# A graph-attention layer with experts: a second gathered row per lane moved into the feature stage, edge flags turned once, and last groups of three and two blocks

## The chip, the cores and the metric

The kernel runs on one core of one Trainium2 chip. The metric is the device time of one execution in microseconds (us), the median over runs. Times inside an execution come from one profiled execution.

## The reference, cut to what matters

Layer normalisation of `x` (30000 x 256), then graph attention over 510,000 edges that are sorted by destination, then a residual sum, and after a second normalisation a shared MLP and four experts of which the best two per row are used. The part that the change touches is the attention:

```python
feat_all = jnp.einsum('ni,rhid->rnhd', inputs, conv_weights)   # 8 relations, 4 heads of 64
feat_src_e = feat_all[edge_type, edge_src]
el = jnp.sum(feat_src_e * attn_l[edge_type], axis=-1)
er = jnp.sum(feat_all[edge_type, edge_dst] * attn_r[edge_type], axis=-1)
e = leaky_relu(el + er, 0.2)
ex = jnp.exp(e - segment_max(e, edge_dst)[edge_dst])
alpha = ex / segment_sum(ex, edge_dst)[edge_dst]
h = segment_sum(alpha[..., None] * feat_src_e, edge_dst)
```

Each edge needs one row of 260 floats (4 heads of 64 features and one attention term), found by its source node and relation.

## The kernel before, in words

The program has two stages; the engines' orders are written out by hand in both (`manual_schedule`), so every engine runs its instructions in the order of the Python loops.

**The feature stage** goes over NT = 235 tiles of 128 nodes. For a tile TensorE makes five column groups (`group`, matmuls L304), ScalarE copies three of them out of PSUM and VectorE two (L306), and SyncE stores the 1 MB of feature rows to `feat` in DRAM (`store`, L318). PSUM holds six such groups. In slots between the groups, `aside` takes one step of a list of side work, `side`: first `edge_records`, then `places`, then `expert_weights`.

`places` goes over the NBLK = 252 blocks of edges in 21 batches of GB = 12. A block has 2048 edges, 128 lanes (partitions) of U = 16 consecutive edges. In each lane the edge with the lowest feature row is found (key, minimum, mark; L534 to L540) and exchanged with the first edge of the lane (L543 to L550); the mark is kept so that the attention stage can exchange the scores alike. `places` also makes the flags of where a destination begins and ends; their ends are turned from partitions into rows by two TensorE instructions a batch (L580, L581), copied by ScalarE (L583) and stored to `thr_d`. A batch takes nine slots; two slots of a tile are used when `places` runs.

`first_rows` then gathers row 0 of every lane of every block early, during the feature stage: one indirect DMA by GpSimd per block (L625), into `fr`, and a plain DMA of three blocks back to DRAM into `stage` (L620). It begins at tile BT + 2 = 178 of 235. The gather may only read `feat` below tile BT = 176; if any lane's lowest row lies above it, a flag makes the program compute everything again in a general form. In the text such a row is called an early row.

**The attention stage** goes over the 252 blocks and one last block of UL = 18 edges a lane. Iteration t has six slots, c = 0 to 5, and works on several blocks: it loads block t + 2 (`load`), gathers block t + 1 (`gather`: SyncE reads row 0 from `stage`, L954, and GpSimd gathers the other 15 rows by 15 indirect DMAs, L956, into a ring `ft` of four blocks), computes the scores of block t in slot 1 (`scores`, L1060 to L1067: add, leaky ReLU, `exchange` L1051 to L1055, two scans) and their softmax in slot 5 (`softmax`, L1092 to L1095 and `exchange` again), and weighs and sums block t - 1 (`weigh` L1109, `sums` L1116, `finish` L1134 to L1137). Between them stand `turn_ends` (TensorE, L987, waits for the scans), `across` (VectorE), `turn_back` (TensorE) and the exponentials (ScalarE, L1101 and L1102).

Every four finished blocks (T = 4) form a group for the experts. Its 22 steps go into a list, `todo`, of which one is taken in each slot: normalise (`spread`, `scale`, L737 to L747), turn (L755), the layers (L811, L836), gates (L763 to L806), and `last` (TensorE L864 to L867, then VectorE adds in the next slot, L870). 253 blocks give 63 groups of four and a last one of a single block.

Of the kernel before, what the change touches and what calls it, by code (L numbers as in the profile page):

```python
# [21 lines left out]
P = 128  # L22
D = 256
R = 8
# [22 lines left out]
WI, WD, WA, WP, W1 = 0, U, 2 * U, 3 * U, 5 * U  # L47
# [9 lines left out]
def kernel(  # L57
# [47 lines left out]
    stage = dram.tile([NBLK * P, H * HW], F32, name="stage")  # L105
# [115 lines left out]
    with ExitStack() as cx:  # L221
# [263 lines left out]
        BT = 3 * NT // 4  # L485
        count = {"ready": 0, "sent": 0}
        low = gp.tile([P, NBLK], I32, name="low")
        lowc = gp.tile([P, NBLK], I32, name="lowc")

        def places(cl):  # L490


            GB = 12
# [14 lines left out]
            rcs = {}  # L508

# [15 lines left out]
            for k, (b0, n) in enumerate(batches):  # L525
# [4 lines left out]
                key = kp.tile([P, GB, U], F32, name="key", bufs=1)[:, :n]  # L530
                km = kp.tile([P, GB], F32, name="km", bufs=1)[:, :n]
                x = rc[:, :, :U, :3].rearrange("p b u f -> p b f u")
                mark = of[:, :, WA:WA + U]
                nc.vector.scalar_tensor_tensor(key, rc[:, :, :U, 0], float(U),  # L534
                                               iu[:, None, :].to_broadcast([P, n, U]), op0=ALU.mult, op1=ALU.add)
                nc.vector.tensor_reduce(km, key, AX.X, ALU.min)
                yield
                if done:
                    done()
                nc.vector.tensor_tensor(mark, key, km[:, :, None].to_broadcast([P, n, U]), op=ALU.is_equal)  # L540
                m3 = mark[:, :, None, :].to_broadcast([P, n, 3, U])
                t3 = kp.tile([P, GB, 3, U], F32, name="t3", bufs=1)[:, :n]
                nc.vector.tensor_mul(t3, x, m3)  # L543
                yield
                for f in range(3):
                    nc.vector.copy_predicated(x[:, :, f, 1:], o[:, :, WA + 1:WA + U],
                                              x[:, :, f, 0:1].to_broadcast([P, n, U - 1]))
                yield
                with nc.allow_low_precision(reason="integers below 2 ** 24"):
                    nc.vector.tensor_reduce(x[:, :, :, 0], t3, AX.X, ALU.add)  # L550
                yield
# [3 lines left out]
                nc.gpsimd.tensor_copy(low[:, b0:b0 + n], rc[:, :, 0, 0])  # L555
                nc.gpsimd.tensor_scalar_min(lowc[:, b0:b0 + n], rc[:, :, 0, 0], float(BT * P * R - 1))
                nc.gpsimd.tensor_copy(o[:, :, WI:WI + U], rc[:, :, :U, 0])
                count["ready"] = b0 + n
# [19 lines left out]

                ps = pf.tile([P, 512], F32, name="ps")[:n, :2 * P]
                nc.tensor.transpose(ps[:, :P], a1[:, :, U - 1], ident)  # L580
                nc.tensor.matmul(ps[:, P:], a2[:, :, 1], turned, start=True, stop=True)  # L581
                thr = kp.tile([GB, 2 * P], F32, name="thr")[:n]
                nc.scalar.copy(thr, ps)  # L583
# [8 lines left out]
                def done(o=o, d16=d16, thr=thr, b0=b0, n=n):  # L592
                    nc.sync.dma_start(thr_d[b0:b0 + n].rearrange("b i p -> b (i p)"), thr)
                    nc.sync.dma_start(rk_d[b0:b0 + n].rearrange("b p w -> p b w"), o)
                    nc.sync.dma_start(dk_d[b0 * CAP:(b0 + n) * CAP].rearrange("(b p u) -> p b u", p=P, u=U), d16)
            yield
            done()

            exc = gp.tile([P, 1], F32, name="exc")
            nc.vector.tensor_reduce(exc, low, AX.X, ALU.max)  # L600
# [6 lines left out]
            yield  # L607
            both = gp.tile([1, 2], F32, name="both")
            nc.vector.tensor_reduce(both[:, 0:1], exr, AX.X, ALU.max)
            nc.vector.tensor_scalar(both[:, 0:1], both[:, 0:1], float(BT * P * R), None, op0=ALU.is_ge)  # L610
# [3 lines left out]
        def first_rows():  # L614

            n, kept = 3, []
            fp = cl.enter_context(tc.tile_pool(name="first", bufs=3))

            def keep(b0, m, fr):
                nc.sync.dma_start(stage[b0 * P:(b0 + m) * P, :].rearrange("(b p) f -> p b f", p=P), fr[:, :m])  # L620
            for b0 in range(0, NBLK, n):
                m = min(n, NBLK - b0)
                fr = fp.tile([P, n, H * HW], F32, name="fr")
                for b in range(m):
                    nc.gpsimd.indirect_dma_start(  # L625
                        out=fr[:, b], out_offset=None, in_=feat[0:BT * P * R, :],
                        in_offset=bass.IndirectOffsetOnAxis(ap=lowc[:, b0 + b:b0 + b + 1], axis=0))
                    if b == n // 2 and kept:
                        keep(*kept.pop())
                    count["sent"] += 1  # L630
                    yield
                kept.append((b0, m, fr))
            while kept:
                keep(*kept.pop(0))

        with tc.manual_schedule():
# [49 lines left out]
            for m in range(lead, NT - 1):  # L686
                for g in range(NG):
# [4 lines left out]
                    if g == 2 or g == 4 and len(side) < 3:  # L692
                        aside()
                    if m >= BT + 2:
                        fetched = min(fetched + 1.03 * NBLK / ((NT - BT - 2) * NG), 3)
                        while fetched >= 1 and count["sent"] < count["ready"]:
                            next(ahead)
                            fetched -= 1
# [176 lines left out]
    with ExitStack() as cx:  # L875
# [170 lines left out]
        def exchange(s, x):  # L1046

            if not s.own:
                return
# [387 lines left out]
```

## Time and profile before

| what | value |
|---|---|
| median of 3 runs | 6604.08 us (6603.03 to 6612.37) |
| the profiled execution | 6606.58 us, of which the span of the instructions is 6604.9 us |
| mean granted TensorE clock | 0.971 |
| TensorE, VectorE, ScalarE, GpSimd busy | 92%, 79%, 52%, 62% of the span |
| last feature matmul (L304) ends | 1741.3 us after the span's start |
| first and last gather of the attention stage (L956) | 1759.2 and 6521.7 us |
| scores of the first and last block (L1060) | 1779.7 and 6524.5 us |

Busy shares are averages over both stages, and matmuls overlap their neighbours in the records, so a TensorE that is busy 9 tenths is not at its peak. An idle time stands with the instruction that follows it, and the releaser is what ended the wait. [...]

### The profile page before, as it was taken

The numbers are of one execution on the slowest core, as the hardware profiler recorded it, in microseconds if no ns is written. First come the engines' busy times: TensorE is split into PE (matmuls) and PEld (weight loads), VectorE is DVE, ScalarE is ACT, GpSimd is POOL, SyncE is SP. The second block draws the span as 40 slices with busy tenths as digits, with TensorE's granted clock in tenths as the row PEclk, the third lists the DMA queues.
The fourth block names the chain that finished last, engine by engine and source line by source line (L and its number), as shares of the span: only waits on it lengthen the run. The fifth ranks groups of instructions, "written<-read, shape, count | busy, mean of one in ns | idle before, by whom it ended". The sixth has DMA issues, their size and how long they took to land. (4 is left out here: it accounts for less than half of the span.)

```text
span 6604.9 us, 97530 instructions
## 1 busy us (share of the span) xinstructions
PE 6063.8 (92%) x25827; PEld 3894.0 (59%) x25828; DVE 5250.5 (79%) x13699; ACT 3411.6 (52%) x8777; POOL 4077.6 (62%) x4382
## 2 busy tenths in 40 slices
PE   9999999999789889999889999999998999989988
PEld 5555555555456666666666666666666666666665
DVE  5555667644488888898888888888888888888885
ACT  2222222222256656666566665666656666666664
POOL 1111111166677777777777777777777777777773
PEclk9999999999899999999999999999999999999999
DMA  6666777799855555555555555555555555555552
GB/s 228 227 208 200 226 238 225 232 342 328 273 159 160 164 165 163 158 163 163 162 167 159 163 163 162 165 161 163 163 161 164 163 163 163 161 164 163 163 160 80
DMA packets 764818, 1214.73 MB, mean 184 GB/s; under 512 B 242730, under 2 KB 603149, under 8 KB 734045
## 3 DMA queue, kind: packets, MB, share of 16 engines
q1 hardware_dynamic: 568813, 668.72, 31.5%
q0 software_dynamic: 194400, 539.40, 29.3%
q8 instruction: 210, 3.44, 0.2%
q14 instruction: 355, 2.91, 0.1%
q10 hardware_dynamic: 1040, 0.26, 0.0%
HBM read 821.54 MB, written 386.43 MB: 183 GB/s over the span
## 5 line engine op out<-in xcount | busy, mean ns | idle before, releaser
L956 POOL DMA_INDIRECT ft<-feat,rk x3798 | 3606.5, 950 | 1168.9 <-issue 396.0
L1116 PE MATMUL po<-ft,oh 128*128 128x260 f32 x8100 | 2197.1, 408 | 139.8 <-DVE ho L1137 130.2
L1116 PEld LDWEIGHTS po<-ft,oh 128*128 128x128 f32 x8100 | 1525.1, 201 | 437.9 <-issue 199.2
L304 PE MATMUL ps<-w,xT 128*128 128x448 f32 (+1 forms) x4700 | 1713.6, 519 | 1.7 <-DMA w<-_L_gnn_conv_weights_dram 1.7
L1109 DVE TENSOR_TENSOR ft<-ft,p 128x768 f32<-128x768 f32 x1518 | 1292.1, 851 | 89.0 <-ACT ft L1102 85.8
L1043 ACT ACTIVATE oh<-icol,rk 128x128 f32<-128x128 f32 x4032 | 1327.9, 389 | 0.0
L304 PEld LDWEIGHTS ps<-w,xT 128*128 128x128 f32 x4700 | 874.0, 190 | 688.0 <-issue 600.2
L306 ACT COPY fo<-ps 128x448 f32<-128x448 f32 (+1 forms) x711 | 378.3, 532 | 1065.2 <-PE ps L304 969.5
L1044 ACT ACTIVATE oh<-oh 128x384 f32<-128x384 f32 x1518 | 741.1, 488 | 48.0
L1020 PEld LDWEIGHTS <-ohT 128*128 128x128 bf16 x4050 | 378.3, 158 | 405.5 <-issue 331.7
L1033 DVE TENSOR_REDUCE e<-ere 128x16 f32<-128x384 f32 (+1 forms) x1012 | 561.3, 555 | 34.6
L1031 DVE TENSOR_TENSOR ere<-pe,rk 128x384 f32<-128x384 f32 x1008 | 550.7, 546 | 1.5 <-PE pe L1020 1.5
L1101 ACT ACTIVATE p<-e 128x64 f32<-128x64 f32 (+1 forms) x253 | 70.2, 277 | 850.0 <-DVE e L1055 839.2
L811 PE MATMUL ph<-xT,v 128*128 128x512 f32 (+1 forms) x1024 | 490.7, 603 | 1.6 <-ACT h L812 1.3
L1020 PE MATMUL pe<-erp,ohT 128*128 128x96 bf16 x4050 | 439.1, 233 | 56.6 <-DVE ohT L1003 55.3
L306 DVE COPY fo<-ps 128x448 f32<-128x448 f32 (+1 forms) x464 | 242.4, 527 | 215.5 <-PE ps L304 212.3
L293 DVE COPY xT<-ptr 128x256 f32<-128x256 f32 x229 | 96.9, 423 | 378.9 <-PE ptr L291 377.1
L625 POOL DMA_INDIRECT fr<-feat,lowc x252 | 239.5, 951 | 191.3 <-DMA stage<-fr 82.4
L1003 DVE TENSOR_SCALAR ohT<-dr,rowid 128x2064 bf16<-128x2064 int16 (+1 forms) x253 | 323.5, 1279 | 0.0
L273 POOL TENSOR_TENSOR xb<-xg,hb 128x1024 f32<-128x1024 f32 (+1 forms) x59 | 142.0, 2406 | 278.3 <-DMA xg<-in_x_dram 144.1
L987 PE MATMUL t<-ident,fb 128*8 128x128 f32 x506 | 103.6, 289 | 205.5 <-DVE fb L1066 205.4
L555 POOL COPY low<-rcb 128x12 int32<-128x12 int32 x21 | 4.1, 197 | 445.3 <-DVE rcb L550 371.2
(217 smaller groups left out, 6979.4 us busy)
## 6 DMA issues: line engine op xcount, KB each, us to landing
feat<-fo SPq DMA_DIRECT2D x234, 1040.0 KB
dr<-dk_d SPq DMA_DIRECT2D x252, 516.0 KB
ft<-feat,rk POOLq DMA_INDIRECT x3798
stage<-fr SPq DMA_DIRECT2D x84, 390.0 KB
ft<-stage SPq DMA_DIRECT2D x252, 130.0 KB
xt<-xb_d SPq DMA_DIRECT2D x253, 128.0 KB
out_dram<-og SPq DMA_DIRECT2D x253, 128.0 KB
xb_d<-xb SPq DMA_DIRECT2D x58, 512.0 KB
```

The costliest lines, as they stand in the source:

```text
L304: nc.tensor.matmul(ps, t["xT"][:, k, :], w[:, k, c0:c1], start=k == 0, stop=k == 1)
L306: eng(t["fo"][:, h0:h1, :HD], ps[:, :n].rearrange("p (a d) -> p a d", d=HD))
L811: nc.tensor.matmul(ps[:, :self.w], lhs, rhs, start=i == 0, stop=i == len(pairs) - 1)
L956: nc.gpsimd.indirect_dma_start(out=s.ft[:, u].rearrange("p h d -> p (h d)"), out_offset=None, in_=feat[:, :], in_offset=bass.IndirectOffse ...
L1003: nc.vector.tensor_scalar(ohT[:, :3 * s.dw].rearrange("n (i e) -> n i e", i=3), s.dr[:, :, :s.dw], rowid[:, t:t + 1], None, op0=ALU.is_equal)
L1020: nc.tensor.matmul(pe[:, u - u0].rearrange("p f r -> p (f r)"), s.ov[:, u, :], s.erp.rearrange("n h k r -> n (h k r)"), start=True, stop=True)
L1031: nc.vector.tensor_mul(ere, s.pe[:, :u1 - u0], s.th[:, u0:u1, None, :].to_broadcast([P, u1 - u0, H * 3, R]))
L1033: nc.vector.tensor_reduce(s.e[:, :, u0:u1].rearrange("p h u -> p u h"), ere.rearrange("p u (h k) r -> p u h (k r)", h=H), AX.X, ALU.add)
L1043: nc.scalar.activation(s.oh[:, u, :], icol, AF.Abs, bias=s.nd[:, u:u + 1])
L1044: nc.scalar.activation(s.oh[:, u0:u1], s.oh[:, u0:u1], AF.Relu, bias=1.0, scale=-1.0)
L1109: nc.vector.tensor_mul(fc, fc, pc[:, :, None].to_broadcast([P, (u1 - u0) * H, HD]))
L1116: nc.tensor.matmul(s.po.rearrange("n h d -> n (h d)"), s.oh[:, u, :], s.ft[:, u].rearrange("p h d -> p (h d)"), start=u == 0, stop=u == s. ...
```

## The change

- **A second early row in every other block.** In blocks with an even number, `places` finds the second lowest row too, exchanges it into place 1 of the lane, and keeps a second mark (16 words more in each row of `rk_d`). `first_rows` gathers 252 first rows and 126 second rows, 378 in all, in pairs (NS = 2), through four buffers of two blocks where there were three of three, and stores each pair as one contiguous piece per partition. It begins at tile FIRST = 141, at a rate that spreads the 378 over the tiles up to the last but one, and the limit on the rows that a gather may read rises with its place (`rows_there`), some six tiles behind the tile then being made.
- In the attention stage an even block reads two rows from `stages` and gathers 14; an odd one reads one and gathers 15. `exchange` is called twice in `scores` and twice in `softmax` for even blocks; for odd ones the second call returns at once.
- **`places` in denser slots.** A batch has 11 steps where it had nine, and three slots of a tile are used where there were two.
- **Ends of the flags turned once.** The two end columns of each batch are copied by GpSimd into `ends`, and turned at the end of `places` by two TensorE instructions for each 128 blocks.
- **Last groups.** The last groups of the experts have three and two blocks where they had four and one, and from iteration 252 on two steps are taken in each slot.
- The zeroing of `fbs` moves from ahead of the attention stage into its iteration 0.

```diff
-WI, WD, WA, WP, W1 = 0, U, 2 * U, 3 * U, 5 * U
+WI, WD, WA, WP, W1 = 0, U, 2 * U, 4 * U, 6 * U
...
-        BT = 3 * NT // 4
+        NF = (NBLK, (NBLK + 1) // 2)
+        FIRST = NT * 3 // 5
+        RATE = 1.02 * sum(NF) / (NT - 1 - FIRST)
+        GB = 12
...
+        def rows_there(i, b0):
+
+            at = b0 - b0 % GB if i == 0 else NBLK + b0 - b0 % (GB // 2)
+            return min(NT - 2, int(FIRST + at / RATE) - 6) * P * R
...
+                nc.gpsimd.memset(o[:, :, WA + U:WA + 2 * U], 0)
+                for i in range(2):
+
+                    v = rc[:, ::i + 1, i:U]
+                    m, w = (n + i) // (i + 1), U - i
...
+                    nc.vector.scalar_tensor_tensor(key, v[:, :, :, 0], float(U),
+                                                   iu[:, None, :w].to_broadcast([P, m, w]), op0=ALU.mult, op1=ALU.add)
+                    nc.vector.tensor_reduce(km, key, AX.X, ALU.min)
+                    yield
...
+                    nc.vector.tensor_tensor(mark, key, km[:, :, None].to_broadcast([P, m, w]), op=ALU.is_equal)
...
+                    nc.vector.tensor_mul(t3, x, mark[:, :, None, :].to_broadcast([P, m, 3, w]))
...
+                    for f in range(3):
+                        nc.vector.copy_predicated(x[:, :, f, 1:], marki[:, :, 1:],
+                                                  x[:, :, f, 0:1].to_broadcast([P, m, w - 1]))
...
+                        nc.vector.tensor_reduce(x[:, :, :, 0], t3, AX.X, ALU.add)
...
-                ps = pf.tile([P, 512], F32, name="ps")[:n, :2 * P]
-                nc.tensor.transpose(ps[:, :P], a1[:, :, U - 1], ident)
-                nc.tensor.matmul(ps[:, P:], a2[:, :, 1], turned, start=True, stop=True)
-                thr = kp.tile([GB, 2 * P], F32, name="thr")[:n]
-                nc.scalar.copy(thr, ps)
+                nc.gpsimd.tensor_copy(ends[:, 0, b0:b0 + n], a1[:, :, U - 1])
+                nc.gpsimd.tensor_copy(ends[:, 1, b0:b0 + n], a2[:, :, 1])
...
+            for b0 in range(0, NBLK, P):
+
+                n = min(P, NBLK - b0)
+                ps = pf.tile([P, 512], F32, name="ps")[:n, :2 * P]
+                nc.tensor.transpose(ps[:, :P], ends[:, 0, b0:b0 + n], ident)
+                nc.tensor.matmul(ps[:, P:], ends[:, 1, b0:b0 + n], turned, start=True, stop=True)
...
+            fp = cl.enter_context(tc.tile_pool(name="first", bufs=4))
...
+            for i, n in enumerate(NF):
+                for b0 in range(0, n, NS):
+                    m = min(NS, n - b0)
+                    fr = fp.tile([P, NS, H * HW], F32, name="fr")
+                    for b in range(m):
+                        nc.gpsimd.indirect_dma_start(
+                            out=fr[:, b], out_offset=None, in_=feat[0:rows_there(i, b0 + b), :],
+                            in_offset=bass.IndirectOffsetOnAxis(ap=lowc[i][:, b0 + b:b0 + b + 1], axis=0))
+                        if b == NS // 2 and kept:
+                            keep(*kept.pop())
...
-                    if g == 2 or g == 4 and len(side) < 3:
+                    if g == 2 or g >= 3 and len(side) == 2:
                         aside()
-                    if m >= BT + 2:
-                        fetched = min(fetched + 1.03 * NBLK / ((NT - BT - 2) * NG), 3)
+                    if m >= FIRST:
+                        fetched = min(fetched + RATE / NG, 3)
...
+                self.early = 2 - t % 2 if self.own else 0
...
-            if s.own:
-                nc.sync.dma_start(s.ft[:, 0].rearrange("p h d -> p (h d)"), stage[t * P:(t + 1) * P, :])
-            for u in range(1 if s.own else 0, s.u):
+            for i in range(s.early):
+                b = t >> i
+                f = b % NS * H * HW
+                nc.sync.dma_start(s.ft[:, i].rearrange("p h d -> p (h d)"), stages[i][b // NS, :, f:f + H * HW])
+            for u in range(s.early, s.u):
...
-        def exchange(s, x):
-
-            if not s.own:
+        def exchange(s, x, i):
+
+            if i >= s.early:
                 return
...
-            exchange(s, s.e)
+            exchange(s, s.e, 1)
+            exchange(s, s.e, 0)
...
-            exchange(s, s.e)
+            exchange(s, s.e, 0)
+            exchange(s, s.e, 1)
...
+        left, sizes = (NBLK + 1) % T, [T] * ((NBLK + 1) // T)
+        sizes = sizes[:-1] + [T - 1, 2] if left == 1 else sizes + [left] if left else sizes[:-1] + [2, 2]
+        member = [(sum(sizes[:q]), n) for q, n in enumerate(sizes) for _ in range(n)]
...
-                    if todo:
-                        after = todo.pop(0)()
-                        if after:
-                            late.append(after)
+                    for _ in range(2 if t >= NBLK else 1):
+                        while late:
+                            late.pop()()
+                        if todo:
+                            after = todo.pop(0)()
+                            if after:
+                                late.append(after)
```

## The prediction

> **What bounds the kernel now.** The page's part 4, the chain that ended last, reaches back only 4 us here, so the bound is read stage by stage. I first read busy time by stretch (columns: time, PE, PEld, DVE, ACT, POOL busy with counts, TensorE clock, DMA share, GB/s).
>
> ```profile
> 1400.00:1600.00 200.00, 200.00 (x604) 108.69 (x603) 92.92 (x279) 51.91 (x111) 128.02 (x127) 1.00 0.97 336
> 2500.00:3500.00 1000.00, 904.00 (x4319) 615.93 (x4318) 889.62 (x2288) 621.84 (x1640) 757.16 (x798) 0.97 0.57 162
> ```
>
> In the feature stage TensorE is never idle; DMA is nearly full once gathers run. In the attention stage no engine looks full. Then the timeline of GpSimd, which shows the bound:
>
> ```profile
> 4000.02 0.94 POOL L956 DMA_INDIRECT ft<-feat,rk  x1 [0.30 <-DVE g L779]
> 4001.27 0.94 POOL L956 DMA_INDIRECT ft<-feat,rk  x1 [0.30 <-PE ph L811]
> 4002.51 0.95 POOL L956 DMA_INDIRECT ft<-feat,rk  x1 [0.30 <-PE po L1116]
> ```
>
> Every gather starts 1.25 us after the one before, whoever is named: the 0.30 us is part of the gather, no wait. From 1759.2 to 6521.7 us the 3798 gathers have a mean spacing of 4762.5/3797 = 1.254 us. GpSimd is the bound: 15 x 1.254 = 18.8 us a block, 75.3 us for the four of an expert group. How near the others are is in the waits of 2500 to 6500 us, which hold 4000/18.81 = 213 blocks, or 53 groups:
>
> ```profile
> DVE e L1060 <- DMA ft<-feat,rk: 79.6, 57, 3.4
> DVE ft L1109 <- ACT ft L1102: 72.8, 55, 2.0
> DVE og L870 <- PE pf L867: 71.3, 106, 1.1
> DVE den L1134 <- PE po L1116: 34.7, 55, 0.6
> ```
>
> VectorE waits for a gather once per group, 79.6/53 = 1.50 us of 75.3. The rest of the cycle is a chain of VectorE and TensorE: without gathers in its way a group would take 75.3 - 1.5 = 73.8 us. Removed gathers can give no more than 2% before this chain is the bound.
>
> **What the skill says.** The Trainium skill, "Perfetto Trace Analysis", section "DMA Instruction — SWDGE (GPSIMD)", says that the shown end of such a DMA is the end of descriptor generation, not of the data movement. The trace agrees: gathers are 0.95 us each while VectorE waits for their data. "VectorE: DVE Perf Modes", section "The TRN2 errata", gives (N + 151)/0.96 ns for an fp32 two-operand operation; N = 64 gives an estimate of 224 ns, and the trace shows 0.22 to 0.23 us for L1051, started 0.26 us apart. So the small exchanges pay a fixed cost that fewer elements won't reduce. "ScalarE: Activation LUTs", section "What ACT_TABLE_LOAD costs", gives 1283 ns; the trace has 1.28 us ahead of L1101, in a wait used below.
>
> **Part 1, the feature stage: -16 us.** TensorE is its bound, so what counts is what leaves TensorE. L580 and L581 take 5.17 + 7.58 = 12.75 us for the 19 batches of 640 to 1350 us, so 14.1 us for 21. Two turns of the same three records each (3 x 0.28 = 0.84 us) come back: -12.4; spans overlap neighbours, I take -11.
>
> VectorE gets the search for the second row. A batch costs now, start to start, 0.53 + 0.35 + 0.38 + 1.15 + 2.36 + 0.73 + 0.54 + 0.33 + 1.2 + 2.1 = 9.7 us (key, minimum, mark, product, three predicated copies, sum, WD, pen, scans, th). The same six kinds on half the blocks: an estimate of 3.2 us. With 11 steps at three a tile a batch lasts 3.67 tiles: 12.9/3.67 = 3.5 us a tile. The rest of a tile is 92.92/200 x 7.31 = 3.4 us (VectorE's share without side work in the stretch shown above; 7.31 us from a tile's first matmul to the next tile's), and it waits 0.36 us for ScalarE's root. Sum 7.3 us, against 7.31 us that TensorE needs: VectorE runs level with TensorE for 77 tiles. Six PSUM buffers hide a lag of some groups; without that cover each 0.1 us a tile costs 8 us. I put it at +3, bounds 0 and +20. GpSimd's added clears and copies (two of 0.1 to 0.5 us a batch) hide in its idle time.
>
> The 378 gathers need 378 x 1.25 = 473 us of GpSimd in 91 tiles x 7.31 = 665 us; before, 252 needed 315 of 402 us besides 82 us of waits for stage writes and 34 us of L273. There GpSimd ended late (last gather 1746.2 us, last matmul 1741.3), SyncE stood behind its stage writes, and the last feature store went out at 1754.3, the first attention gather at 1759.2. With slack that tail of 17.9 us should shrink to about 10 (copy and issue 2 to 4, plus the 4.9 from last store to first gather seen now): -8, bounds 0 and -10. DMA share goes from 0.97 to about 0.59 + 0.38 x 4.15/4.55 = 0.94, more while `places` still runs; stores have six tiles, 44 us, before a gather waits for them. The moved clears of `fbs` (one waits 16.7 us today) lie under the first block's gathers: nothing.
>
> **Part 2, the start of attention: -5 us.** Block 0 has 14 gathers: -1.25. Scores of blocks 0 to 6 go at GpSimd's pace, as no expert work is there yet; six blocks at 14.5 instead of 15 give 6 x 0.63 = -3.8.
>
> **Part 3, the steady groups: +20 us.** GpSimd now needs 58 x 1.254 = 72.7 us a group, below the chain's 73.8, so the gather wait goes (-1.5) and the chain is late next. Four blocks hold two even ones, each with two more exchanges:
>
> ```profile
> 4076.61 0.23 DVE L1051 TENSOR_TENSOR m<-e,rk 128x64 f32<-128x64 f32 x1
> 4076.87 0.23 DVE L1053 COPY_PREDICATED e<-rk,e 128x60 f32<-128x60 int32 x1
> 4077.14 0.22 DVE L1055 TENSOR_REDUCE e<-m 128x4 f32<-128x64 f32 x1
> 4077.39 0.29 DVE L1066 TENSOR_TENSOR_SCAN fb<-pens,e 128x64 f32<-128x64 f32 x1
> ```
>
> From L1051 to what follows is 0.78 us, so 4 x 0.78 = 3.12 us a group. What of it do waits take up? In iteration 4q + 2 (experts' layers) `turn_ends` waits for the scans (0.41 us at 4077.74), so the 0.78 in `scores` delays TensorE by 0.78; TensorE then runs without a gap to `sums`' end. VectorE, 1.56 late, eats its wait there:
>
> ```profile
> 4091.18 0.16 DVE L1134 TENSOR_SCALAR den<-po 128x4 f32<-128x4 f32 x1 [0.64 <-PE po L1116]
> ```
>
> Net 1.56 - 0.63 = +0.93. The next iteration has no VectorE wait and passes it on. In iteration 4q (the `last` steps) TensorE comes to `turn_ends` about 0.68 us after the scans let it (scan at 4039.95, TensorE at 4040.77), so of the 0.78 only 0.10 reaches it; VectorE then waits for `last` anyway:
>
> ```profile
> 4043.54 0.42 DVE L870 TENSOR_TENSOR og<-pf,x 128x256 f32<-128x256 f32 x1 [1.09 <-PE pf L867]
> 4058.00 0.27 DVE L1060 TENSOR_TENSOR e<-e,ft 128x64 f32<-128x64 f32 x1 [0.94 <-DMA ft<-feat,rk]
> ```
>
> So +0.10 there, and +0.78 in its softmax, where nothing waits. ScalarE's wait in iteration 4q + 1 (L1109, 1.4 us, the table load) starts from VectorE's own L743 and stays. Sum 0.93 + 0.10 + 0.78 - 1.50 = +0.3 us a group; 61 groups: +20. Bounds: all 3.12 added, +1.6 a group, +100; everything but VectorE's own work absorbed, -2 a group. SyncE's 126 more reads of `stages` are issued over a block ahead: nothing.
>
> **Part 4, the end: -7 us.** Block 252's scores wait 3.85 us for their 18 gathers; GpSimd will be ahead: -3.9. Two `last` steps in slot 0 put one of 2.6 us ahead of its scores, half of it hidden: +1.3. From the last scores to the span's end are now 80.4 us; after `finish` (6548.5) the group of four runs alone for 28 us and the single block for 21. With three and two blocks the first group's 18 us of steps lie beside the last sums, but these are TensorE's too: I count 42 us to `finish` instead of 24, then 28 for the group of two with 6.9 behind it, 76: -4, bounds -15 and +5.
>
> **Sum.** -16 - 5 + 20 - 7 = -8 us: 6599 on the profiled execution's 6606.58 us (span 6604.9 and 1.7 around it). The median of the runs is 2.5 lower, so 6604 - 8 = 6596 us, no change: 0.2%, 13 us, is about what a measurement of this kernel can tell from none.
>
> **Rivals.** (a) *Slower, 6676:* the waits of VectorE don't shrink, because TensorE and ScalarE shift with it; then every exchange counts, +1.6 a group, +100 in place of +20. Place: L1051 to L1055 of even blocks. It turns the sum to slower by over 0.2% once a group loses (28 + 13)/61 = 0.7 us net. For it: ScalarE's wait starts from VectorE. Against: the wait for `sums` at L1134 is behind a TensorE that was only 0.78 late. (b) *Slower, 6620:* `places` makes VectorE the bound of the features: +20, and no shorter tail. For it: 7.3 against 7.31. Against: TensorE had no wait there. (c) *Faster, 6450:* VectorE's other waits vanish too and a group takes 70.1 (VectorE's own: 75.3 less 5.0 of waits) + 3.1 = 73.2 us; 61 x 2.4 below part 3: -146. Against: ScalarE's table load stays. A third of it (49 us) gives 6547. (d) The limit on rows trips and everything is computed twice: with the reference's inputs the highest row asked for is 31,570 rows below its limit, so no.
>
> **Chances.** Forecast 0.62 (faster 0.25, same 0.26, slower 0.11; own range 6570 to 6622), (a) 0.12, (b) 0.10 (same 0.03), (c) 0.04 and a third of it 0.12. Together: faster 0.41, same 0.29, slower 0.30. The range 6545 to 6645 takes in the forecast, (b) and the third of (c), and leaves out (a) and (c) in full, 0.16.
>
> **What would show it.** Right: gaps between L956's successors over 0.3 us, no wait of `scores` for gathers, groups of 75.6 us; first attention gather near 1743; scores of block 0 near 1762 and of the last block near 6520. Wrong: group length under 74.5 or over 76.5, TensorE idle in the features, or the gathers still 1.25 us apart throughout.

## The result and the profile after

| | before | after |
|---|---|---|
| median | 6603.56 us (6601.18 to 6612.37, 4 runs) | 6646.21 us (6641.85 to 6651.48, 4 runs) |
| span of the profiled execution | 6604.9 us | 6645.9 us |

The ratio is 1.0064, with a 95% interval of 1.0051 to 1.0076: the change makes the kernel 43 us slower. The forecast was 6596 us in a range of 6545 to 6645, so the time lies just above the range; slower had a chance of 0.30.

Where the 41 us of the spans come from, by four marks of the two traces:

| stretch | before | after | difference |
|---|---|---|---|
| start to the end of the last feature matmul | 1741.3 | 1802.6 | +61.3 |
| from there to the scores of block 0 | 38.4 | 23.3 | -15.1 |
| scores of block 0 to scores of the last block | 4744.8 | 4735.2 | -9.7 |
| from there to the end | 80.4 | 84.8 | +4.4 |

The feature stage has lost more than everything else has won. The busy times by stretch of the kernel after show where (columns as before: time, PE, PEld, DVE, ACT, POOL busy with counts, TensorE clock, DMA share, GB/s):

```profile
1045.00:1254.00 209.00, 166.12 (x445) 86.35 (x445) 114.69 (x301) 36.30 (x82) 101.94 (x141) 0.89 0.87 282
1400.00:1600.00 200.00, 200.00 (x603) 108.74 (x602) 93.30 (x283) 51.40 (x109) 126.47 (x124) 1.00 0.97 346
2500.00:3500.00 1000.00, 889.85 (x4320) 608.32 (x4319) 923.15 (x2450) 616.95 (x1626) 731.30 (x772) 0.99 0.57 164
```

From 1400 us on the features run as before, with TensorE full. Between 1045 and 1254 us TensorE stands 43 of 209 us; before, it was busy there throughout:

```profile
1045.00:1254.00 209.00, 209.00 (x637) 112.23 (x636) 144.75 (x373) 54.61 (x118) 35.22 (x67) 1.00 0.74 236
```

VectorE and ScalarE do less in it than before, not more, so neither is full. This is the stretch in which `places` still runs and the early gathers have begun (tile 141 starts at 1056.9 us). TensorE's waits in it, each with its total, how often it came and the longest, sum to the 43 us:

```profile
PE ps L307 <- DVE xT L296: 21.7, 7, 6.5
PE ps L307 <- ACT thr L624: 9.2, 1, 9.2
PE ps L621 <- POOL endsk L600: 7.7, 1, 7.7
PE ptr L294 <- DVE a_xn L149: 4.3, 1, 4.3
```

(`xT` is VectorE's copy of the turned rows, `thr` ScalarE's copy of the turned flags, `endsk` GpSimd's copies of the ends of the flags, `a_xn` the normalised rows.)

The attention stage answers to the lines of before like this; first GpSimd's timeline, which has room now:

```profile
4014.43 0.94 POOL L996 DMA_INDIRECT ft<-feat,rk  x1 [0.30 <-issue]
4018.78 0.95 POOL L996 DMA_INDIRECT ft<-feat,rk  x1 [3.42 <-DVE ere L1071]
4020.03 0.94 POOL L996 DMA_INDIRECT ft<-feat,rk  x1 [0.30 <-issue]
```

Once in a group of four, at the first gather of its last block, GpSimd now waits for a free place in the ring: 3.42 us here, and 53 such waits between 2500 and 6500 us. The last `sums` matmul of the block that held the place (L1159) ends at 4018.09 us; the profile names an instruction of VectorE that ends at 4018.71. So GpSimd is no longer the bound. VectorE's waits of 2500 to 6500 us:

```profile
DVE ft L1152 <- ACT ft L1145: 68.5, 53, 1.5
DVE og L907 <- PE pf L904: 39.5, 108, 0.4
DVE e L1101 <- DMA ft<-feat,rk: 0.7, 3, 0.3
```

The wait for a gather has gone from 79.6 to 0.7 us, the one for `pf` from 71.3 to 39.5, and the one for `po` is not in the list any more. Both exchanges of an even block, in its scores:

```profile
4005.53 0.22 DVE L1093 TENSOR_TENSOR m<-e,rk 128x60 f32<-128x60 f32 x1
4005.78 0.23 DVE L1095 COPY_PREDICATED e<-rk,e 128x56 f32<-128x56 int32 x1
4006.05 0.22 DVE L1096 TENSOR_REDUCE e<-m 128x4 f32<-128x60 f32 x1
4006.30 0.23 DVE L1093 TENSOR_TENSOR m<-e,rk 128x64 f32<-128x64 f32 x1
```

The second row's exchange (60 elements) takes 0.77 us, the first's 0.78: as forecast, fewer elements save nothing. A group of four takes 75.13 us; before, 75.28.

### The profile page after: what moved, and what is told of

Same layout as the page of the kernel before. It is cut to its first block, busy times and chain, and to the rows that moved or that the text cites. A ratio compares the mean times of both kernels' runs of the same rounds, so it can differ in the third digit from the quotient of the medians.

```text
span 6645.9 us, 98513 instructions
## 1 busy us (share of the span) xinstructions
PE 6016.5 (91%) x25770; PEld 3860.3 (58%) x25771; DVE 5472.3 (82%) x14625; ACT 3406.5 (51%) x8758; POOL 4106.4 (62%) x4487
## 5 line engine op out<-in xcount | busy, mean ns | idle before, releaser
L996 POOL DMA_INDIRECT ft<-feat,rk x3672 | 3481.8, 948 | 1277.5 <-issue 403.0
L1159 PE MATMUL po<-ft,oh 128*128 128x260 f32 x8100 | 2150.2, 401 | 185.8 <-DMA xt<-xb_d 142.2
L1159 PEld LDWEIGHTS po<-ft,oh 128*128 128x128 f32 x8100 | 1497.2, 197 | 475.0 <-issue 252.7
L307 PE MATMUL ps<-w,xT 128*128 128x448 f32 (+1 forms) x4700 | 1730.3, 523 | 38.8 <-DVE xT L296 27.6
L307 PEld LDWEIGHTS ps<-w,xT 128*128 128x128 f32 x4700 | 882.5, 192 | 740.0 <-issue 638.5
L660 POOL DMA_INDIRECT fr<-feat,lowc x378 | 360.1, 953 | 283.9 <-DMA stage<-fr 190.9
L848 PE MATMUL ph<-xT,v 128*128 128x512 f32 (+2 forms) x1024 | 490.3, 602 | 0.5 <-ACT a L849 0.5
L848 PEld LDWEIGHTS ph<-xT,v 128*128 128x128 f32 x1024 | 185.9, 191 | 144.0 <-issue 132.1
L903 PE MATMUL pf<-v,a 128*128 128x256 f32 x1012 | 260.9, 380 | 7.6 <-issue 5.6
```

Source lines behind the costliest of these rows:

```text
L307: nc.tensor.matmul(ps, t["xT"][:, k, :], w[:, k, c0:c1], start=k == 0, stop=k == 1)
L660: nc.gpsimd.indirect_dma_start(out=fr[:, b], out_offset=None, in_=feat[0:rows_there(i, b0 + b), :], in_offset=bass.IndirectOffsetOnAxis(ap ...
L848: nc.tensor.matmul(ps[:, :self.w], lhs, rhs, start=i == 0, stop=i == len(pairs) - 1)
L996: nc.gpsimd.indirect_dma_start(out=s.ft[:, u].rearrange("p h d -> p (h d)"), out_offset=None, in_=feat[:, :], in_offset=bass.IndirectOffse ...
L1159: nc.tensor.matmul(s.po.rearrange("n h d -> n (h d)"), s.oh[:, u, :], s.ft[:, u].rearrange("p h d -> p (h d)"), start=u == 0, stop=u == s. ...
```

## The chain behind the loss

A tile's start is the start of each twentieth feature matmul (L307, before L304). Undisturbed, 20 tiles take 146.2 us. The same table serves the experiments:

| us for the tiles | 80 to 140 | 140 to 160 | 160 to 234 | last feature matmul starts |
|---|---|---|---|---|
| before | 447.4 | 148.9 | 542.9 | 1740.8 |
| after | 448.9 | 209.6 | 541.0 | 1802.1 |

In tiles 140 to 160 the chain around GpSimd's longest stall reads as follows. SyncE's own timeline:

```profile
1132.71 1.32 SPq L653 DMA_DIRECT2D stage<-fr  x2
1134.96 13.32 SPq L530 DMA_DIRECT2D rcb<-rec  x12
...
1149.30 1.06 SPq L253 DMA_DIRECT2D xg<-in_x_dram  x1
1150.46 1.32 SPq L653 DMA_DIRECT2D stage<-fr  x1
```

`fetch` has SyncE load the records of the next 12 blocks. For 13.32 us it issues nothing else, and no stage write goes out from 1134 to 1150 us. GpSimd, at the same time:

```profile
1142.58 1.08 POOL L660 DMA_INDIRECT fr<-feat,lowc  x1 [0.30 <-issue]
1157.90 0.96 POOL L660 DMA_INDIRECT fr<-feat,lowc  x1 [14.24 <-DMA stage<-fr]
```

It has filled its four buffers of two blocks and stands 14.24 us until a stage write has landed. VectorE and TensorE:

```profile
1156.42 0.43 DVE L142 BATCH_NORM_STATS2 a_st<-xg 128x6 f32<-128x256 f32 x1 [9.23 <-DMA xg<-in_x_dram]
```

```profile
1158.09 0.69 PE L294 MATMUL ptr<-ident,a_xn 128*128 128x128 f32 x2 [4.27 <-DVE a_xn L149]
```

The load of the next nodes' `x` stood behind the fetches too and went out at 1149.30; VectorE waits for it until 1156.42, and TensorE for the normalised rows. This one chain costs TensorE 4.27 of its 43 us. What SyncE's order costs in all is not read from a single chain but from the experiments below. The Trainium skill, "Perfetto Trace Analysis", section "DMA Instruction — HWDGE (DVE, Sync)", says that the profile shows such a DMA only until its sequencer is free, not the movement of its data; the trace agrees: the load is shown for 1.06 us, and VectorE's wait ends 7.1 us after the load's start. What makes a fetch dear is not the DMA's issue. Twelve take 13.32 us, 1.11 each, and the issue is 0.33 of that:

```profile
L530 SPq DMA_DIRECT2D rcb<-rec x12: 332/333/343, 1135.0 to 1147.9; - x12
L528 SPq TENSOR_LOAD <-lo_sb x11: 263/268/669, 1135.3 to 1147.2; - x11
L528 SPq FUSED_REGOPS  x12: 147/147/154, 1134.5 to 1147.5; - x12
```

Ahead of each issue SyncE loads the block's first edge from SBUF into a register (0.27 us) and runs a few register instructions (0.15 us for the longest); the rest are shorter ones and gaps between them. The timeline leaves these out, and so shows one long row. The kernel before fetches in the same way, with nothing in a hurry behind it:

```profile
1051.87 13.55 SPq L518 DMA_DIRECT2D rcb<-rec  x12
```

This chain was not my first reading; it became one (theory F) when theories A to E, which the experiments name, had all fallen short.

## The experiments

Each time stands beside the 6646 us of the kernel after, unless said otherwise; the kernel before took 6603.6 to 6609.2 us beside these runs. The runs e9 to e15 and e18 were made on chips where the attention stage of the kernel before, too, took over 100 us a group in place of 75, so from these only the feature stage and the end are used; tiles go at the same 7.31 us there. (The kernel before was not traced on them; this is read from its times of 8510 to 8527 us and from the trace of e15.)

**e1, e2, e3, e4: is it the overlap, and which link of it?**

```diff
-        FIRST = NT * 3 // 5
+        FIRST = 158
```

> The changed kernel with one number other: the early gathers begin at tile 158 instead of 141, after the search (places) has ended near tile 154. Theory A (the loss comes from the overlap: clears and copies of places stand on GpSimd's queue behind gathers that wait for stage writes, VectorE waits for them, TensorE for VectorE): tiles 140 to 160 come back to 7.3 us each, 63 us less, about 6585. Theory B (VectorE is too full with the second search, wherever the gathers lie): the search is where it was, so no change, 6646. Theory C (only the single buffer of thr, whose second copy waits for a store queued behind stage writes): 17 to 25 us less, 6621 to 6629.

6665.85 us, slower still. But tiles 140 to 160 took 164.7 us, 45 less than after: the overlap is what costs there. What was won came back as a larger loss: tiles 160 to 234 took 591.7 us for 541.0, and from the last feature matmul to the scores of block 0 it took 39.8 us for 23.3. The waits of 1370 to 1800 us show it, VectorE's, then SyncE's:

```profile
DVE a_st L142 <- DMA xg<-in_x_dram: 97.3, 13, 9.6
```

```profile
SPq L653 <- DMA fr<-feat,lowc: 272.1, 93, 6.8
```

At 5.1 gathers a tile SyncE stands at its stage writes for 272 us, and VectorE 97 us for loads of `x`, which go out on the same queue. The kernel after, at 4.1 a tile, has 203.4 us of the first in this stretch, none of the second, and a TensorE that is full. So none of the three theories had the total; A had the place right.

```diff
-                thr = gp.tile([P, 2 * P], F32, name="thr")[:n]
+                thr = gp.tile([P, 2 * P], F32, name="thr", bufs=2)[:n]
```

> The changed kernel with two buffers for thr, so that the second turn's copy doesn't wait 24.7 us for the first one's store. Theory A: at most 10 us less, 6636 to 6646. Theory B: no change, 6646. Theory C: 17 to 25 us less, 6621 to 6629.

6636.33 us. The 9.2 us that TensorE waited for the second copy of `thr` are a separate loss of 10 us, and the change's own: turned once, the second copy needs the buffer that SyncE stores late.

```diff
+            rko = [kp.tile([P, GB, WR], I32, name=f"rko{i}", bufs=1) for i in range(2)]
+            for t in rko:
+                nc.gpsimd.memset(t[:, :, WA + U:WA + 2 * U], 0)
...
-                o = kp.tile([P, GB, WR], I32, name="rko")[:, :n]
+                o = rko[k % 2][:, :n]
...
-                nc.gpsimd.memset(o[:, :, WA + U:WA + 2 * U], 0)
```

> The changed kernel with two fixed rko buffers whose second marks are cleared once, so that no clear of a batch stands on GpSimd's queue ahead of VectorE's mark. Theory A, if the clear is the link between the queue and VectorE: 20 to 45 us less, 6601 to 6626. Theory B: no change (at most 3 us), 6646. Theory C: no change.

6649.56 us: no gain. TensorE's waits only change their names; two that were 4.3 and 7.7 us in 1045 to 1254 us of the kernel after are its longest now:

```profile
PE ptr L294 <- DVE a_xn L149: 15.3, 1, 15.3
PE ps L623 <- POOL endsk L602: 15.0, 1, 15.0
```

and VectorE waits 18.39 us for a load of `x`. The clear was a link, not the cause.

```diff
                 for i in range(2):
-
+                    if i == 1:
+                        yield
+                        yield
+                        continue
...
-                    nc.gpsimd.tensor_scalar_add(low[i][:, c0:c0 + m], v, float(-most))
+                    nc.gpsimd.tensor_scalar_add(low[i][:, c0:c0 + m], v, float(-most) - 1e6)
```

> The changed kernel without VectorE's search for the second row (its steps are empty, the second mark stays zero, and the second gathers fetch whatever record stands second, so the features of even blocks' second rows are other ones); 378 gathers, GpSimd's clears and all pacing stay. Theory A: the clears still stand behind gathers, so most of the loss stays: 0 to 20 us less, 6626 to 6646. Theory B: 50 to 73 us less, 6573 to 6596. Theory C: no change.

6645.26 us. Without the search of VectorE nothing is won; theory B, which is rival (b), falls.

**e5, e6, e7: bytes, or the wait for the gather at the write?** (e7 has the edits of e2 and e5.)

```diff
-                        if b == NS // 2 and kept:
-                            keep(*kept.pop())
+                        if b == NS // 2 and len(kept) > 1:
+                            keep(*kept.pop(0))
...
-                    while kept:
+                    while len(kept) > 1:
                         keep(*kept.pop(0))
```

> The changed kernel with each stage write put on SyncE's queue one pair of gathers later, so that its gather has had some 2.5 us more to land; bytes and buffers as they were (GpSimd has one pair less before it needs the buffer again). Theory D (bytes: gathers, stage writes, and the records of places together ask more of the DMA engines than they move, so that loads of x and stores land late): no change, within 8 us of 6646. Theory E (order: SyncE's queue stands at each stage write until the gather lands, and the loads and stores behind it go out late): 20 to 50 us less, 6596 to 6626.

6657.57 us, 11 slower, of which 4 are in the features and 6 between them and the first attention gather (10.2 us for 4.0): a write's gather had more time, but SyncE still waited 54.6 us for gathers in 1045 to 1254 us (55.7 after), and GpSimd, with a buffer less in reserve, 78.2 us for writes (71.3). Neither theory foresaw a loss.

```diff
-                nc.sync.dma_start(stages[i][b0 // NS, :, :m * H * HW], fr[:, :m].rearrange("p b f -> p (b f)"))
+                k = m * H * HW if b0 == 0 else 16
+                nc.sync.dma_start(stages[i][b0 // NS, :, :k], fr[:, :m].rearrange("p b f -> p (b f)")[:, :k])
...
-                nc.sync.dma_start(s.ft[:, i].rearrange("p h d -> p (h d)"), stages[i][b // NS, :, f:f + H * HW])
+                nc.sync.dma_start(s.ft[:, i].rearrange("p h d -> p (h d)"), stages[i][0, :, f:f + H * HW])
```

> The changed kernel with stage writes of 64 bytes a partition instead of 2080 (the first pair of each list is written in full, and attention reads that pair for every block, so the early rows' features are wrong); the same number of writes and the same waits for gathers. This takes 133 KB of 266 KB from each gather's traffic. Theory D: the loss of the features goes for the most part, 40 to 63 us less, 6583 to 6606. Theory E: at most 15 us less, 6631 to 6646, since SyncE still stands at each write until its gather has landed.

6634.48 us, and tiles 140 to 160 in 198.3 us. Half of the gathers' traffic is gone and 11 of 63 us come back: bytes have a share, a small one. Theory D falls as the main cause.

> The two edits of e2 and e5 together (thr in two buffers, stage writes one pair later). If they act on separate waits, the gain of e5 and the 10 us of e2 add up: theory D 6630 to 6640, theory E 6586 to 6616.

6656.46 us, 1 us less than e5: the two don't add up. What remained was that GpSimd stood 71 to 81 us for stage writes in e5, e7 and in the kernel after, and 61 us where the writes were tiny (e6). Writes so short that still come so late have to be issued late, which led to SyncE's timeline and to theory F.

**e9, e10, e12: the fetches spread.**

```diff
                 for b in range(n):
+                    if b > 1:
+                        yield
...
-                fetch(k + 1)
+                more = fetch(k + 1)
+                next(more, None)
...
+                    next(more, None)
                     yield
```

> The changed kernel with the twelve record fetches of a batch of places (1.11 us of SyncE each, 13.4 us in one go) spread over the batch: two at its start, one more at each step, the rest at its end. Theory F (while SyncE issues the twelve, no stage write goes out; after four pairs GpSimd has no buffer and stands up to 14 us, with the clears, copies and xb of the others behind it, and the load of x goes out late; VectorE and then TensorE wait): most of the 63 us of tiles 140 to 160 comes back, 40 to 60 us less, 6586 to 6606. Theory A in its wider form (gathers and GpSimd's own clears and copies in one queue, however SyncE is loaded): 0 to 12 us less, 6634 to 6646.

> The edit of e9 with thr in two buffers. Theory F: another 5 to 10 us less than e9, since the second copy's wait for the first store stays without it. Theory A wider: as e2, 6636 or a little less.

> The same kernel as e10 (fetches spread, thr in two buffers), to have its whole time beside the kernel before at that one's usual clock. Theory F, from its feature stage (last feature matmul at 1750.7 us against 1802.1): 6646 - 51 = 6595. If the 51 us are lost again in the attention stage: 6620 to 6646.

> As e10, but with two fetches at each step, so that a batch's records are there by its sixth step of eleven (in e10 VectorE waited 11.3 us for the last of them). Theory F: 5 to 12 us less than e10_again, 6583 to 6590. If stage writes are held back again by pairs of fetches (2.2 us), 0 to 10 us more.

| us for the tiles | 80 to 140 | 140 to 160 | 160 to 234 | last feature matmul starts |
|---|---|---|---|---|
| e9, spread | 438.6 | 180.7 | 541.0 | 1761.6 |
| e10, with `thr` in two buffers | 438.7 | 168.7 | 541.0 | 1750.7 |
| e10 again | 438.6 | 170.3 | 541.9 | 1752.6 |
| e12, two fetches a step | 438.7 | 179.4 | 542.0 | 1762.5 |

Spreading alone takes 40.5 us off the end of the features (1802.1 to 1761.6), and `thr` another 9 to 11. It also takes 10 us from tiles 80 to 140, where no gather runs: there too loads stood behind the fetches (VectorE waited 12.2 us for `x` in 590 to 1045 us of the kernel after). SyncE's timeline of the second run of e10 shows stage writes after every three fetches:

```profile
1083.13 2.88 SPq L532 DMA_DIRECT2D rcb<-rec  x3
1086.13 0.36 SPq L667 DMA_DIRECT2D stage<-fr  x1
1086.59 0.40 SPq L321 DMA_DIRECT2D feat<-fo  x1
1087.10 0.40 SPq L667 DMA_DIRECT2D stage<-fr  x1
1088.86 3.28 SPq L532 DMA_DIRECT2D rcb<-rec  x3
1092.25 0.36 SPq L667 DMA_DIRECT2D stage<-fr  x1
```

Two at a step lost 10 us again (the second case of its expectation). The whole times of e9, e10 and e12 (8306 to 8315 us beside 8510 to 8512 for the kernel before) say nothing of the usual ones; that was for e17.

**e13 and e15: what is left, and whether the kernel before had it.**

> As e12, with the early gathers from tile 147 on, at 4.4 a tile for 4.1. If the rest of the loss in tiles 140 to 160 is the overlap itself, 8 to 15 us less than e12, 6570 to 6580. If the denser gathers run into what stopped e1 (5.1 a tile: tiles of 8.6 us late in the stage), as much as e12 or more, up to 6620.

With gathers from tile 147 on, tiles 140 to 160 take 163.7 us, 16 less than e12, but 160 to 234 take 553.9, 12 more: last matmul at 1757.7. The first attention gather comes at 1775.8 us, 8.8 later than in e12 (1767.0). The overlap has a price of its own, and so has the denser pace; 141 is not a bad start.

> The kernel before with the record fetches spread over the steps of a batch (one more a step), nothing else. If fetches on SyncE also cost the kernel before its 12 us of tiles 80 to 180: 9 to 12 us less, 6592 to 6595. If those 12 us are the turns of the flags, as the prediction had it: no change, 6604.

Last matmul at 1743.2, tiles 80 to 140 in 448.6 us: no gain. The kernel before wasn't held back by its fetches, and the 10 us between its 448.6 and the 438.6 of e10 are the turns, as forecast: L580 and L581 are busy for 9.0 us of this stretch in the kernel before.

**e16 and e17: the fetches off SyncE.** In e16 all of them are issued by ScalarE, in e17 only those from batch 16 on, which overlap the gathers (and `thr` has two buffers, the rest spread as in e10):

```diff
+                late, act = k >= 16, mybir.EngineType.Activation
...
-                    lo = nc.values_load(lo_sb[0:1, b0 + b:b0 + b + 1], engines={SP}, min_val=0, max_val=E)
+                    lo = nc.values_load(lo_sb[0:1, b0 + b:b0 + b + 1], engines={act if late else SP}, min_val=0, max_val=E)
...
-                    nc.sync.dma_start(rc[:, b].rearrange("p u f -> p (u f)"),
+                    (nc.scalar if late else nc.sync).dma_start(rc[:, b].rearrange("p u f -> p (u f)"),
```

> As e10, with the spread fetches issued by ScalarE instead of SyncE: 13.4 us of SyncE free in each batch, at the price of as much on ScalarE, one fetch a step. Theory F to the full (SyncE's time is what the overlap lacks): tiles 140 to 160 within 10 us of the 146 they take undisturbed, last feature matmul at 1730 to 1742; 6575 to 6587 where the attention stage has the usual clock. If the overlap costs by itself: tiles 140 to 160 as in e10 (168 to 170 us), last matmul near 1751. If ScalarE's copies of PSUM come late behind the fetches: TensorE waits for them, last matmul above 1760.

6605.55 us beside 6609.21, which is no difference (ratio 0.9994, interval 0.9985 to 1.0003). Tiles 140 to 160 in 161.5 us, 7 to 9 less than e10, but not within the 10 us of 146 that theory F to the full asked for; tiles 80 to 140 in 444.9 us, 6 more than e10, and the last feature matmul only at 1759.1, later than in e10. ScalarE's own work now stands behind its fetches: in 590 to 1045 us VectorE waits 46.1 us for ScalarE's root, 22.4 in the second run of e10.

> As e10 up to batch 15 of 21 (fetches spread, on SyncE), and as e16 from batch 16 on (on ScalarE), so that SyncE is free of fetches where the gathers overlap the search. Theory F, adding up both: tiles 80 to 140 in 439 us, tiles 140 to 160 in about 162, last feature matmul at 1742 to 1746, and where the attention stage has its usual clock 6585 to 6592, 0.2 to 0.3% less than the kernel before. If e16's gain in the overlap came from its being late in the first part: last matmul near 1751 as in e10, 6595.

6591.84 us beside 6608.61, ratio 0.9976 with an interval of 0.9968 to 0.9983: 54 us less than the change as given (59 if each is taken against the kernel before that ran beside it), and 0.2% faster than the kernel before. The parts add up: tiles 80 to 140 in 440.2 us, 140 to 160 in 161.0, last matmul at 1746.7 us. The stretch that lost 43 us of TensorE loses 11.6:

```profile
1045.00:1254.00 209.00, 197.45 (x587) 105.89 (x586) 134.00 (x358) 47.73 (x110) 128.73 (x161) 0.98 0.95 312
```

What remains, 15 us in tiles 140 to 160, comes with 0.95 of the DMA engines in use, GpSimd waiting 45.9 us for writes and SyncE 80.4 us for gathers. Whether it is bytes or order wasn't told apart.

**e8: the price of the second exchange.**

```diff
-            exchange(s, s.e, 1)
             exchange(s, s.e, 0)
...
             exchange(s, s.e, 0)
-            exchange(s, s.e, 1)
```

> The changed kernel without the exchanges of the second row in scores and softmax (the second early row is not swapped back, so sums of blocks with a second row are wrong); gathers and everything else stay. It measures what the exchanges cost in the steady groups, put at 1.8 us a group in the prediction (0.93 + 0.10 + 0.78), 61 groups: 110 us less, 6536. If VectorE and TensorE absorb them (waits of the group shrink by as much), 0 to 40 us less; if every exchange counts, 3.12 us a group, 190 us less, 6456.

6584.29 us, 62 less, which is 1.0 us for each of 61 groups. In the traces a group takes 74.27 us where the kernel after takes 75.13: by these the exchanges cost 0.86 us a group, half of the 1.8 that was forecast. VectorE's waits of 2500 to 6500 us, in e8:

```profile
DVE ft L1150 <- ACT ft L1143: 81.1, 61, 2.0
DVE og L907 <- PE pf L904: 74.6, 107, 1.1
DVE den L1179 <- PE po L1157: 42.2, 68, 0.7
DVE c L1133 <- PE t L1127: 20.4, 14, 1.5
```

They sum to 218 us in 53.9 groups, 4.05 a group; after, all of VectorE's waits sum to 110 us in 53.2 groups, 2.07 a group. So waits give way by 1.98 us of the 3.12 that the exchanges take, which leaves 1.14, near the 0.86 measured.

**e11 and e18: the last groups.**

```diff
-        sizes = sizes[:-1] + [T - 1, 2] if left == 1 else sizes + [left] if left else sizes[:-1] + [2, 2]
+        sizes = sizes + [left] if left else sizes
...
-                    for _ in range(2 if t >= NBLK else 1):
+                    for _ in range(1):
```

> The changed kernel with the groups of before (62 of four and a single block last, one expert step a slot at the end). The prediction had the new groups shorten the end from 80.4 to 76: then this one is 4 us slower, 6650. The trace showed the end at 84.8: if the new groups lengthened it (two last steps in one slot hold VectorE and TensorE one behind the other), it is 4 us faster, 6642; if the second early row or the clock did, no change.

> The kernel of e17 with the groups of before (62 of four, then a single block; one step a slot at the end). If the new groups lengthen the end: from the last scores to the span's end 80 to 81 us, as before, and 4 us less in all than e17, 6588. If they shorten it as forecast and something else lengthened it: 88 us, 6596. If they make no difference, 84 us, 6592.

From the last scores to the end: 83.5 us in both with the old groups; with the new ones 82.7 to 87.6 on such chips (e9 to e13), and 82.4 to 87.2 in the other runs. A trace of one execution can't show 4 us here. The mean of the 16 traces with the new groups is 84.5 us, of the four with the old ones 82.5 (80.4 before, 82.6 in e15). So the gain of 4 us to 76 is in no trace, and whether the new groups cost something stays open.

## Why the prediction was wrong

The sum missed by 50 us, and a part of the miss is hidden: up to the last feature matmul the kernel took 61 us more where 8 less were forecast, and the steady groups gave back 26 us of it by taking less than forecast. The prediction's own sign of being wrong, "TensorE idle in the features", is what came.

- **The bound and its views: right.** GpSimd was the bound of the attention stage. Without the gathers in its way, and without second exchanges, a group takes 74.27 us (e8), forecast 73.8.
- **Part 1, turned once, -11: right in kind and size.** Tiles 80 to 140 take 438.6 us with it and 448.6 without, both with fetches spread: -10. But its copy of `thr` brought a wait of 10 us back (e2), which the step did not price.
- **Part 1, VectorE, +3 with bounds 0 and +20: its low end.** Without the search the loss stays (e4), and with it and spread fetches tiles 80 to 140 take 438.6 us, the undisturbed pace. 7.3 us against 7.31 were level, as forecast, and the search is not what made VectorE late.
- **Part 1, the failed step.** The step that moves the gathers to tile 141 priced GpSimd ("GpSimd's added clears and copies (two of 0.1 to 0.5 us a batch) hide in its idle time"), the DMA share and the landing of feature stores; nothing priced SyncE's queue in that stage, which is to put it at nothing without a reason. But each pair of gathers puts a stage write on SyncE, and where the gathers overlap `places` SyncE also makes twelve fetches of 1.11 us at a stretch. Measured: +61 us in tiles 140 to 160, 209.6 for the 148.9 of before. Of them 29 are the fetches in a row (180.7 in e9), 8 to 9 more the time that spread fetches still take on SyncE there (161.0 in e17 for 168.7 to 170.3 in e10), 10 to 12 are `thr` (e9 to e10), and 12 are left (161.0 for 148.9), whose cause stays open. Ahead of the overlap the same fetches, now every 27 us for every 33, ate the 10 us of the turns. The prediction read 82 us of GpSimd waits for stage writes in the kernel before, and took them for a lack of GpSimd's time.
- **Part 1, the shorter tail, -8: more than that, and beyond its bound of -10.** From the last feature matmul to the first attention gather 17.9 us became 4.0.
- **Part 2, -5: right.** Block 0's scores come 19.3 us after the first gather, before 20.5 (-1.2); the next six blocks take 109.96 us for 113.06 (-3.1).
- **Part 3, +20: the wrong sign.** The gather wait went, as said, and GpSimd got its gaps. The exchanges' term was mis-sized, 0.86 us a group for 1.8, as more of VectorE's waits shrank than the two that were followed. A group takes 0.15 us less, not 0.3 more.
- **Part 4, -7: did not come.** Block 252's wait of 3.85 us for its gathers is gone, as said, but the last two blocks' scores take 39.24 us for 39.39 all the same. The end took 4.4 us more, which lies within what single executions of these kernels differ by (82.4 to 87.6 us); 76 was in none.
- **The rivals.** (a) is refuted, since the waits shrink by 1.98 us a group; (b) had the right stage and sign, and the wrong engine; (c) did not come, which needed groups of 73.2 us, as a group takes 74.27 even without the second exchanges; (d) did not happen.

## What to carry to other kernels

When work is moved into another stage, write down what it puts on each queue there, SyncE's among them, and in which order: here a loop of twelve loads with addresses from registers held SyncE for 13 us, and what stood behind it handed that on. When an edit to the engine that waits changes only the names of the waits (e3) or nothing (e4), follow the wait back to who issues what it waits for. And an overlap that is stretched away (e1) can cost more as a denser pace later than it saved; first thin out what collides.

## What the runs showed of the hardware that was not expected

- A plain DMA whose address is loaded into a register first occupies SyncE for 1.11 us: 0.33 us for the issue, 0.27 for the load of the register from SBUF, 0.15 for the longest of the register instructions, the rest shorter ones and gaps (twelve in 13.32 us; 13.55 us in the kernel before).
- An overlap at 0.87 of the DMA engines' time on the mean (282 GB/s) lost TensorE 43 of 209 us, and one at 0.95 (312 GB/s, e17) only 11.6: the share did not tell which of the two was in trouble.
- On some chips the attention stage took 102 us a group with the change and 105 without (e9, e15), for 75 elsewhere, while the feature stage took the same; there the kernel before took 8510 to 8527 us and the changed ones 8306 to 8356. VectorE, TensorE and GpSimd had pauses of 4 to 20 us there whose releaser no record names. The granted TensorE clock in 3500 to 5500 us was 0.85 to 0.86 there, for 0.99 to 1.00 in the kernel after. What the pauses are was not tried. There the changed kernels were 1.9 to 2.5% faster than the kernel before, e11 among them, which differs from the change as given in its last groups alone (8355.6 for 8511.7 us). So that the change makes the kernel slower is shown for the chips with 75 us a group alone.
